# A decoder layer whose token blocks are turned by VectorE and DMA in place of TensorE

## The chip, the core and the metric

The kernel runs on one core of one Trainium2 chip. The metric is the device time of one execution in microseconds (us), as the median of several runs. The kernel before took 3067.01 us (three runs, 3065.17 to 3067.51).

A core has five engines with instruction queues of their own: TensorE (PE in the profile; its weight loads are PEld), VectorE (DVE), ScalarE (ACT), GpSimd (POOL) and SyncE (SP, which here only issues DMAs). They meet through semaphores. Sixteen DMA engines carry out what SP, ACT and POOL issue. SBUF is the on-chip memory, with 128 partitions; PSUM is the memory that TensorE writes its products to, in banks.

## The reference: what is computed

One decoder layer in float32, with layer normalization after each part. `x` has 32 sequences of 64 tokens with 512 features, so 2048 tokens.

```python
x = _layernorm(x + attn(x, ...))            # 32 heads on 8 key/value heads of 128; keys and values: 512 gathered
                                            # cache rows and the 64 tokens of the first sequence
x = _layernorm(x + xattn(x, ctx_4096, ...)) # each sequence attends to its own 64 context tokens
z = x @ W.T + b                             # feed-forward with 8 experts of rank 16, folded into one product
m = einsum(x, A, B, p_scores)
x = _layernorm(z + minimum(0.5 * norm(z) / (norm(m) + 1e-6), 1.0) * m)
```

## The kernel before

**Tokens and blocks.** The 2048 tokens are four blocks (`tb`, 0 to 3) of 512. A block is held twice. `acc[tb]` has tokens on the partitions: `[128, 4, 512]`, four row groups `j` of 128 tokens with 512 features each; token `j * 128 + p` of the block lies on partition `p` (`rows`, L111). The turned copy, `xTs` in the first stage and `xT[tb]` (x1T) later, has features on the partitions: `[128, 4, 512]`, four feature groups `c` of 128 and 512 tokens each. TensorE contracts over partitions, so each product that reads x needs the turned copy. The first one is laid out on the host (`xT_in`). x after the first and after the second normalization (x1 and x2) has to be turned on the chip.

**How x is turned before.** `transpose_rows` (L125) takes one row group: four TensorE transposes of 128x128 into one PSUM bank (L129), and a copy of 128x512 to the turned tile by ScalarE or VectorE (L131).

**Stages.** (1) *Self attention* (`scores`, `move`, `values`; to about 1830 us). (2) *Keys and values of the context* (L986 to L1031): 15 pairs `(gp, tb)` of two heads and one block. Each pair is a product of seven steps in the order `KV_ORDER = (1, 6, 5, 7, 2, 4, 3)`. A step is 12 matmul groups into the banks x, y or z (L395 to L410), of which there are two sets, taken in turn; `read` then lets VectorE add what a step left (L417). Steps 6, 7 and 4 add up in the same bank y, and each of their partial sums is read before the next is added. After each step one entry of the list `fill` is issued (L1017), which spreads other work over the pair: for `gp == 1` the statistics and the scaling of the first normalization, for `gp == 2` the four turned row groups of x1, one behind each of the first four steps. After the pair, `store_kv` writes two 512 KB tiles to DRAM (L472); these tiles have two buffers. (3) *Cross attention*: 32 units `(g, tb)` of four heads and one block. Unit `n` issues its queries, turns its weights with VectorE's 32x32 transposes (L1104) and eight DMAs that move the 32x32 blocks between partitions (`move`, L1118), and in the next iteration `attend` multiplies them with the values (`pox`, L1139) and empties four PSUM banks into `oT` with the value bias added (ScalarE L1157, VectorE L1159, four instructions of 128x256 each). `output_sums` on GpSimd (L266) and the output product `wx` (L292) read `oT`. (4) *Feed-forward*: `feed_forward(tb)` (L1193), woven in at the end. Its weight loads take 128 token columns of `xT[tb]` and of `uT` (L1204, L1210, L1211).

**x2.** When the last unit of a block is projected (L1171), its statistics are taken, ScalarE scales it (L167), and `transpose_block` goes to the list `later`, which is emptied between step 2 and step 4 of the next queries (L1298). Blocks 0 and 1 fall into the iterations of units 30 and 31, blocks 2 and 3 into the time after them.

**What sets the order.** In stage 2 TensorE and VectorE run in the order in which the code issues (`manual_schedule`, L990); in stage 3 TensorE, GpSimd and VectorE do, without VectorE from the last unit on (L1277). Elsewhere a planner orders an engine's instructions by priority. Semaphores are set by the framework: an instruction waits until what it reads is written and until what it overwrites has been read, and a tile of a tag with one buffer is handed on when all uses of the one before it are over.

```python
for i in KV_ORDER:                 # L1014
    pr.step(i)                     # TensorE
    pr.read()                      # VectorE: the additions of this step
    if fill:
        fill.pop(0)()              # one entry of other work
```

Of the kernel before, what the change touches and what calls it, by code (L numbers as in the profile page):

```python
# [9 lines left out]
F32 = mybir.dt.float32  # L10
I32 = mybir.dt.int32
AF = mybir.ActivationFunctionType
ALU = mybir.AluOpType
# [3 lines left out]
P = 128  # L17
DIM = 512
NH, NKV, HD = 32, 8, 128
REP = NH // NKV  # L20
NT = 2048
SEQ = 64
TB = 512
NTB = NT // TB
TPB = TB // P
NC = DIM // P
# [5 lines left out]
SQ = 32  # L32
NQD = P // SQ
# [19 lines left out]
def decoder_layer(  # L53
# [30 lines left out]
    nc = tc.nc  # L84
# [12 lines left out]

    acc = [act.tile([P, TPB, DIM], F32, tag=f"acc{b}", name=f"acc{b}") for b in range(NTB)]  # L100
    xT = []

# [6 lines left out]
        )  # L109

    def rows(src, tb):  # L111
        return src[tb * TB : (tb + 1) * TB, :].rearrange("(j p) f -> p j f", p=P)


    psum = []
# [17 lines left out]
    def transpose_block(tb, name):  # L133
        for j in range(TPB):
            transpose_rows(acc[tb][:, j, :], xT[tb], j, f"{name}_{tb}_{j}")

    def layernorm(tb, name):
        for part in layernorm_parts(tb, name):
# [47 lines left out]
    HF = DIM // 2  # L186
# [290 lines left out]
    later = []  # L477


    with ExitStack() as ph:  # L480
# [4 lines left out]
        sb = ph.enter_context(tc.tile_pool(name="sa", bufs=2))  # L485
# [76 lines left out]
        def rotate(g, t0=0, t1=NKT):  # L562
# [14 lines left out]
            nc.gpsimd.tensor_tensor(k4[:, :, :, 1], k4[:, :, :, 1], tmq, ALU.subtract)  # L577
            nc.vector.tensor_tensor(k4[:, :, :, 0], k4[:, :, :, 0], tmp, ALU.add)

        x64 = kc.tile([P, NC, SEQ], F32, name="x64")  # L580

        def new_keys(g):

            wk, wv = wkv_cur.pop(g)
            src = xTs[0] if g == 0 else x64
            kTs[g] = kv.tile([P, NKEY], F32, tag="kT", name=f"kT{g}")
            new = bank([P, 1, TB], f"new{g}", "po1")[:, 0, :]
            pk, pv = new[:, :SEQ], new[:, P : 2 * P]  # L590
            for c in range(NC):
                nc.tensor.matmul(
                    pk, wk[:, c, :], src[:, c, :SEQ], start=(c == 0), stop=(c == NC - 1),
                    skip_group_check=True,
                )
            for c in range(NC):
                for i in range(2):
                    nc.tensor.matmul(
                        pv[i * SEQ : (i + 1) * SEQ, :], src[:, c, :SEQ], wv[:, c, :],
                        start=False, stop=(c == NC - 1), skip_group_check=True,  # L600
                    )
            nc.scalar.activation(
                kTs[g].rearrange("p (s b k) -> p s b k", s=2, k=SQ)[:, :, SHARED, :],
                pk.rearrange("p (s k) -> p s k", s=2), AF.Copy, scale=nrm2,
            )
            nc.scalar.copy(vs[g][:, NKT, :], pv)
# [169 lines left out]
        t = {i: big.tile([P, 2, HF], F32, tag=f"tx{i}", name=f"tx0_{i}") for i in range(1, 5)}  # L776
        for j in range(NKT):
            gather_keys(0, j)
        nc.vector.tensor_tensor(t[1], q[0, 1], q[0, 0], sub)
        nc.vector.tensor_tensor(wq0[7], wq0[1], wq0[5], sub)  # L780
        nc.vector.tensor_tensor(wq0[5], wq0[5], wq0[4], ALU.add)
# [13 lines left out]
        c = first.c  # L795
# [9 lines left out]
        for j in range(NKT):  # L805
            gather_values(0, j)
        cached_keys(0, "s0")
        nc.gpsimd.tensor_copy(x64, xTs[0][:, :, :SEQ])
        nc.vector.tensor_tensor(t[3], q[1, 1], q[0, 1], sub)
        nc.vector.tensor_tensor(t[4], q[1, 0], t[2], sub)  # L810
        tok[1] = token_sums(xTs[1], "tx1", nc.gpsimd)
# [151 lines left out]
    with ExitStack() as ph:  # L963
# [23 lines left out]
        with ExitStack() as st:  # L987
            ke = st.enter_context(tc.tile_pool(name="ke", bufs=1))
            psum.append(st.enter_context(tc.tile_pool(name="kps", bufs=1, space=PSUM)))
            st.enter_context(tc.manual_schedule(  # L990
                engines={mybir.EngineType.PE, mybir.EngineType.DVE}
            ))
            for tb in range(2, NTB):
                encT[tb] = ke.tile([P, NC, TB], F32, tag=f"encT{tb}", name=f"encT{tb}")
                load_features(encT[tb], encT_in, tb)
            kvw[1] = load_kv_left(1, "wo")
            fill, turns = [], [0]

            def rows_turn(src, dst, j, name):
                transpose_rows(src, dst, j, name, f"t{turns[0] % 2}")  # L1000
                turns[0] += 1

            pairs = [(gp, tb) for gp in range(NKV // 2) for tb in range(NTB)][1:]
            for k, (gp, tb) in enumerate(pairs):
                if gp == 1:
                    stats, scale = layernorm_parts(tb, "a")
                    fill += [lambda: None, stats, lambda: None, scale]
                if gp == 2:
                    fill += [lambda tb=tb, j=j: rows_turn(
                        acc[tb][:, j, :], xT[tb], j, f"x1_{tb}_{j}") for j in range(TPB)]  # L1010
                tiles = [ke.tile([P, 2, 2, HF], F32, tag=f"c{i}", name=f"c{gp}_{tb}_{i}", bufs=2)
                         for i in range(2)]
                pr = keys_values(gp, tb, tiles, {z: f"{z}{k % 2}" for z in "xyz"})
                for i in KV_ORDER:  # L1014
                    pr.step(i)
                    pr.read()
                    if fill:  # L1017
                        fill.pop(0)()
                if gp == 0 and tb < NTB - 1:
                    encR[tb + 1] = token_sums(  # L1020
                        encT[tb + 1], f"te{tb + 1}", nc.gpsimd, ke, f"te{tb + 1}_"
                    )
                store_kv(gp, tb, tiles)
                if tb == NTB - 1 and gp < 2:
                    kvw[gp + 2] = load_kv_left(gp + 2, ("wq", "wo")[gp])
                if tb == NTB - 1 and gp == 2:
                    load_xq(0)
                if gp == 3 and tb == 0:
                    right[0] = token_sums(xT[0], "txx0", nc.gpsimd)
            load_xo(0)  # L1030
            psum.pop()  # L1031
# [92 lines left out]
        def attend(n):  # L1124

            g, tb = units[n]
            oTs[n] = output_tiles(f"oTx{g}_{tb}")
            o5 = [o.rearrange("d h (t b q) -> d t b h q", t=TPB, b=2) for o in oTs[n]]
            po = {}
            for pr in range(2):  # L1130
                for b in range(2):
                    name = f"pox{g}_{tb}_{pr}_{b}"
                    po[pr, b] = (bank([P, 2, REP * SEQ], name) if pr else
                                 pp.tile([P, 2, REP * SEQ], F32, tag=f"po{b}", name=name))
                for i in range(2):
                    for b in range(2):
                        r = slice(b * SEQ, (b + 1) * SEQ)
                        t = 2 * pr + i
                        nc.tensor.matmul(  # L1139
                            po[pr, b][:, i, :].rearrange("d (h a j) -> d h a j", h=REP, a=2),  # L1140
                            kvs[n][r, pr, 1, i * HD : (i + 1) * HD],
                            pTs[n][r, :, t * P : (t + 1) * P].rearrange(
                                "p a (h j) -> p h a j", h=REP
                            ),
                            start=True, stop=True,
                        )

            bias = bv[:, g : g + 1]
            for pr in range(2):
                for j in range(2):  # L1150
                    for b in range(2):
                        dst = o5[j][:, 2 * pr : 2 * pr + 2, b, :, :]
                        src = po[pr, b][:, :, j * HF // 2 : (j + 1) * HF // 2].rearrange(
                            "d i (h q) -> d i h q", h=2
                        )
                        if b == 0:
                            nc.scalar.activation(dst, src, AF.Identity, bias=bias)  # L1157
                        else:
                            nc.vector.tensor_scalar(dst, src, bias, None, ALU.add)  # L1159
            left = output_sums(oTs.pop(n), f"sox{g}_{tb}")  # L1160
            pjs[n] = Projection(left, wo_cur[g], tb, f"wx{g}_{tb}", XYZ)
            del pTs[n], kvs[n]

        def project(n, *steps):
            g, tb = units[n]
            for i in steps:
                pjs[n].step(i)
                pjs[n].read()
            if steps[-1] == 4:
                del pjs[n]  # L1170
                if g == NKV - 1:  # L1171
                    stats, scale = layernorm_parts(tb, "x", by_act=True)
                    stats()
                    scales.append(scale)
                    later.append(lambda: transpose_block(tb, "x2"))


        def load_ffn():
# [14 lines left out]
        def feed_forward(tb):  # L1193
# [7 lines left out]
            nc.vector.tensor_scalar(uT, pu, pe, None, ALU.mult)  # L1201
            for i in range(TPB):
                u = f"{tb}_{i}"
                cols = slice(i * P, (i + 1) * P)  # L1204
                a = acc[tb][:, i, :]
                pz = bank([P, DIM], f"pz{u}")
                pm = bank([P, DIM], f"pm{u}")
# [19 lines left out]
                nc.vector.tensor_scalar(gam, gam, CLAMP, 1.0, ALU.mult, ALU.min)  # L1227
                nc.vector.scalar_tensor_tensor(a, pm, gam, a, ALU.mult, ALU.add)
                layernorm_tile(tb, i, "f")
                r0 = tb * TB + i * P  # L1230
                nc.sync.dma_start(out=out[r0 : r0 + P, :], in_=a)

        def next_tokens(n, part):

# [163 lines left out]
```

## Time and profile before

| what | value |
|---|---|
| median of the runs | 3067.01 us |
| the profiled execution | 3067.85 us |
| its span, first to last instruction | 3066.1 us |
| TensorE busy, matmuls | 3028.1 us, 99% |
| VectorE / ScalarE / GpSimd busy | 2171.1 / 766.4 / 961.1 us |
| mean granted TensorE clock | 0.999 |
| DMA: queue of SP | 186224 packets, 280.60 MB, 33.2% of 16 engines |
| transposes of x1 and x2 on TensorE (L129) | 128, 1937.4 to 3032.2 us |
| copies out of their banks (L131) | ACT 0.585 to 0.617 us, DVE 0.680 to 0.682 us each in stage 2 |

An engine is "busy" while an instruction of it runs; matmuls overlap, so the sum of their durations is more than the time in which they are issued, and their slots are read from their start times. A line of a timeline gives start and length in us, engine, line of the code, operation, the tiles (written `out<-in`), the shape, and how many in a row (x4); a bracket is the idle time of that engine before it and what ended it. TensorE's instructions in float32 come in two passes, so a matmul of the code counts twice (a transpose counts once). "SPq" lines are DMA issues on SyncE's queue; their length runs from the first issue to the end of the last.

### The profile page before, as it was taken

To read this page: it belongs to the slowest core of one execution; us is meant where nothing else is said; L and a number is where in the kernel's file an instruction comes from. 1 tells how busy PE (TensorE), PEld (TensorE's weight loads), DVE (VectorE), ACT (ScalarE), POOL (GpSimd) and SP (SyncE) were. 2 spreads that over 40 slices of the span, in tenths; PEclk is the share of its full clock that TensorE was granted. 3 is DMA by queue.
4 is the path that set the end of the run, shared out by engine and by line. 5 is a ranking of instruction groups with operands and counts; after the bars stand their busy time and mean duration, and the time that the engine had idled before them with its cause. 6 is when DMAs were issued, how large, how long until landed. Compare 5 with 4: busy or idle time off the path is not lost.

```text
span 3066.1 us, 42299 instructions
## 1 busy us (share of the span) xinstructions
PE 3028.1 (99%) x14944; PEld 2317.9 (76%) x14944; DVE 2171.1 (71%) x3945; ACT 766.4 (25%) x1776; POOL 961.1 (31%) x789
## 2 busy tenths in 40 slices
PE   8999999999999999999999999999999999999998
PEld 6677777777767777777777769988888888888864
DVE  7787787777877877877877764436666656666677
ACT  2323222222322233232222221211111111111232
POOL 4221321321321321322322123036434444444421
PEclk9999999999999999999999999999999999999999
DMA  5444444444344354344344343231121121121101
GB/s 173 128 132 129 109 116 128 107 122 119 104 125 118 102 130 119 101 128 120 101 125 113 91 129 141 99 108 50 55 62 52 52 66 51 51 69 49 49 28 42
DMA packets 201105, 298.66 MB, mean 97 GB/s; under 512 B 44352, under 2 KB 95040, under 8 KB 200896
## 3 DMA queue, kind: packets, MB, share of 16 engines
q1 hardware_dynamic: 186224, 280.60, 33.2%
q10 hardware_dynamic: 12624, 11.16, 1.3%
q0 software_dynamic: 2048, 4.20, 0.5%
q8 instruction: 120, 1.97, 0.3%
q14 instruction: 89, 0.73, 0.1%
HBM read 107.05 MB, written 20.97 MB: 42 GB/s over the span
## 4 chain that ended last, share of the span: by engine, by line
PE 91%; DVE 4%; SPq 2%; DMA 1%; ACT 1%; issue 1%; ACTq 0%; DVEq 0%
PE po L677 15%; PE s L631 14%; PE sx L1068 2%; PE pox L1139 2%; SPq L669 2%; PE wx_2y L292 1%; PE w_0y L292 1%; PE wx_1y L292 1%; PE wx_0y L292 1%; PE w_3y L292 1%; PE qx_3y L292 1%; PE qx_2y L292 1%; PE qx_0y L292 1%; PE q_2y L292 1%; PE wx_3y L292 1%; PE qx_1y L292 1%
## 5 line engine op out<-in xcount | busy, mean ns | idle before, releaser
L639 ACT ACTIVATE p<-s,nmax 128x576 f32<-128x576 f32 x512 | 379.1, 741 | 1244.9 <-DVE nmax L636 1234.8
L631 PE MATMUL s<-kT,qT 128*128 128x288 f32 x2048 | 576.5, 407 | 5.0 <-ACT p L639 4.2
L677 PE MATMUL po<-pT,v 128*128 128x512 f32 (+1 forms) x1280 | 549.0, 602 | 6.4 <-DMA pT<-T 6.0
L631 PEld LDWEIGHTS s<-kT,qT 128*128 128x128 f32 x2048 | 387.2, 190 | 108.0 <-issue 18.7
L636 DVE TENSOR_REDUCE nmax<-s 128x1 f32<-128x576 f32 x512 | 384.1, 750 | 59.2 <-PE s L631 59.2
L657 DVE STREAM_TRANSPOSE T<-p 128x576 f32<-128x576 f32 x512 | 394.2, 770 | 4.9 <-DVE nmax L636 0.5
L677 PEld LDWEIGHTS po<-pT,v 128*128 128x128 f32 (+1 forms) x1280 | 213.3, 189 | 206.5 <-issue 177.8
L649 DVE TENSOR_SCALAR p<-p,den 128x576 f32<-128x576 f32 x512 | 319.9, 625 | 17.9
L648 DVE RECIPROCAL den<-den 128x1 f32<-128x1 f32 x512 | 83.9, 164 | 230.0 <-ACT p L639 219.9
L266 POOL TENSOR_TENSOR so<-oT,oT 128x512 f32<-128x512 f32 x32 | 40.7, 1271 | 553.0 <-ACT oT L700 553.0
L268 POOL TENSOR_TENSOR so<-oT 128x512 f32<-128x512 f32 x32 | 40.6, 1270 | 346.2 <-ACT oT L700 95.7
L1247 POOL TENSOR_TENSOR txx<-x1T 128x512 f32<-128x512 f32 x31 | 39.3, 1267 | 229.9 <-PE qx_3z L292 93.2
L207 POOL TENSOR_TENSOR tx<-xT 128x512 f32<-128x512 f32 x31 | 39.6, 1278 | 206.3 <-PE q_3z L292 65.0
L639 ACT ACTIVATION_READ_ACCUMULATOR p<-s,nmax 128x1 f32 x512 | 98.7, 193 | 0.0
L266 POOL TENSOR_TENSOR sox<-oTx,oTx 128x512 f32<-128x512 f32 x32 | 40.5, 1265 | 181.5 <-DVE oTx L1159 176.0
L1085 ACT ACTIVATE ex<-ex 128x512 f32<-128x512 f32 x64 | 39.3, 630 | 203.2 <-DVE ex L1084 203.2
L1068 PEld LDWEIGHTS sx<-kvx,qTx 128*64 128x64 f32 x2048 | 62.3, 138 | 10.6 <-issue 10.6
L700 ACT COPY oT<-po 128x512 f32<-128x512 f32 x128 | 68.2, 587 | 4.7 <-PE po L677 3.8
L1157 ACT ACTIVATE oTx<-pox,bv 128x256 f32<-128x256 f32 x128 | 52.0, 470 | 66.4 <-PE pox L1139 66.4
L1068 PE MATMUL sx<-kvx,qTx 128*64 128x64 f32 x2048 | 66.7, 224 | 0.0
L1139 PE MATMUL pox<-pTx,kvx 64*128 64x256 f32 x512 | 64.6, 389 | 0.0
L1159 DVE TENSOR_SCALAR oTx<-pox,bv 128x256 f32<-128x256 f32 x128 | 53.6, 479 | 9.9 <-PE pox L1139 9.9
(447 smaller groups left out, 5767.6 us busy)
## 6 DMA issues: line engine op xcount, KB each, us to landing
pT<-T SPq DMA_DIRECT2D x1016, 80.0 KB
pT<-T SPq DMA_DIRECT2D x1008, 64.0 KB
xT<-in_xT SPq DMA_DIRECT2D x31, 1024.0 KB
kvx<-kv SPq DMA_DIRECT2D x32, 512.0 KB
pTx<-Tx SPq DMA_DIRECT2D x256, 64.0 KB
kv<-c SPq DMA_DIRECT2D x30, 512.0 KB
wo<-in_woT SPq DMA_DIRECT2D x32, 256.0 KB
xwq<-in_xwq SPq DMA_DIRECT2D x32, 256.0 KB
```

The lines of the kernel that those rows point to most:

```text
L266: nc.gpsimd.tensor_tensor(t[1], a[1, 0], a[1, 1], ALU.add)
L292: nc.tensor.matmul(self.banks[b][:, m, :], self.left[i][:, k, m * P : (m + 1) * P], self.right[i][:, k, :], start=(first and m + k == 0), ...
L631: nc.tensor.matmul(s[:, a, :HALF], qTs[n // REP][:, units[n][2], i * P : (i + 1) * P], kTs[g][:, a * HALF : (a + 1) * HALF], start=True, s ...
L636: nc.vector.tensor_reduce(nmax, s[:, :, :HALF], AX.XY, ALU.max, negate=True)
L639: nc.scalar.activation(p.rearrange("q (a k) -> q a k", a=2), s[:, :, :HALF], AF.Exp, bias=nmax, accum_out=den,)
L648: nc.vector.reciprocal(den, den)
L649: nc.vector.tensor_scalar(p, p, den, None, ALU.mult)
L657: nc.vector.transpose(Ts[n][:, :, i, :], ps_.pop((n, i)).rearrange("q (b k) -> q b k", k=SQ))
L677: nc.tensor.matmul(pos[n].rearrange("d (a q) -> d a q", a=NQD), vs[units[n][0]][rows, v, :], pTs[n // 2][rows, :, chunk, :], skip_group_ch ...
L700: nc.scalar.copy(o[:, i, :].rearrange("d (t a k) -> d a t k", t=TPB, a=NQD), pos.pop(n - 1 + i).rearrange("d (a t k) -> d a t k", a=NQD, t ...
L1068: nc.tensor.matmul(s[b * SEQ : (b + 1) * SEQ, i * REP + h, :], qTs[n][:, h, pr * HF + c0 : pr * HF + c0 + SEQ], kvs[n][:, pr, 0, c0 : c0 + ...
L1139: nc.tensor.matmul(po[pr, b][:, i, :].rearrange("d (h a j) -> d h a j", h=REP, a=2), kvs[n][r, pr, 1, i * HD : (i + 1) * HD], pTs[n][r, :, ...
```

## The change

- **Token order.** A partition of `acc` now holds four tokens that follow each other: token `4 * p + j` of the block is on partition `p` in row group `j` (`rows`). The host lays out `xT_in` in the order (j, p) to match, the output DMA writes by `rows`, and `x64`, the first sequence's 64 tokens, is picked out of the new order; it is now copied before the first use of it (group 0 read `xTs[0]` directly before).
- **x1, all four blocks.** `rows_turn` is replaced. Each row group is turned by one VectorE transpose of 32x32 blocks into a tile `room` `[128, 16, 32, 4]`, at every fourth element (`turn_rows`). When the four groups are in, sixteen DMAs on SyncE's queue move 32 partitions each to 32 partitions of x1T, four pieces of 512 bytes a partition (`move_rows`, 64 KB each). The fifth entry of `fill` issues them. `room` comes from the pool `ke`, whose tiles have one buffer.
- **x2, blocks 0 and 1.** The same, with a `room` of one buffer in the pool of stage 3. Blocks 2 and 3 are still turned by TensorE.
- **x1T and x2 of blocks 0 and 1** are thereby in the plain token order, x2 of blocks 2 and 3 in the order (j, p). So `attend` has to write `oT` in the order (j, p): each eviction is split in two, 16 instructions of 128x128 in place of 8 of 128x256 per unit, and each writes with a step of 128 elements. `feed_forward` loads its weights from every fourth column for blocks 0 and 1.

```diff
     def rows(src, tb):
-        return src[tb * TB : (tb + 1) * TB, :].rearrange("(j p) f -> p j f", p=P)
+        return src[tb * TB : (tb + 1) * TB, :].rearrange("(p j) f -> p j f", p=P)
...
+    def turn_rows(src, room, j):
+        nc.vector.transpose(room[:, :, :, j], src.rearrange("p (b f) -> p b f", f=SQ))
+
+    def move_rows(room, dst):
+        blocks = room.rearrange("f (c r) t j -> f r c (t j)", r=NQD)
+        for a in range(NQD):
+            for r in range(NQD):
+                nc.sync.dma_start(
+                    out=dst[r * SQ : (r + 1) * SQ, :, a * P : (a + 1) * P],
+                    in_=blocks[a * SQ : (a + 1) * SQ, r, :, :],
+                )
...
-            src = xTs[0] if g == 0 else x64
...
+        nc.gpsimd.tensor_copy(
+            x64.rearrange("p c (j k) -> p c j k", j=TPB),
+            xTs[0].rearrange("p c (j k) -> p c j k", j=TPB)[:, :, :, : SEQ // TPB],
+        )
...
                 if gp == 2:
-                    fill += [lambda tb=tb, j=j: rows_turn(
-                        acc[tb][:, j, :], xT[tb], j, f"x1_{tb}_{j}") for j in range(TPB)]
+                    room = ke.tile([P, DIM // SQ, SQ, TPB], F32, tag="room", name=f"room{tb}")
+                    fill += [lambda tb=tb, j=j, room=room: turn_rows(
+                        acc[tb][:, j, :], room, j) for j in range(TPB)]
+                    fill.append(lambda tb=tb, room=room: move_rows(room, xT[tb]))
...
-            o5 = [o.rearrange("d h (t b q) -> d t b h q", t=TPB, b=2) for o in oTs[n]]
+            o5 = [o.rearrange("d h (q t b k) -> d t b h k q", t=TPB, b=2, q=TPB) for o in oTs[n]]
...
-                        dst = o5[j][:, 2 * pr : 2 * pr + 2, b, :, :]
-                        src = po[pr, b][:, :, j * HF // 2 : (j + 1) * HF // 2].rearrange(
-                            "d i (h q) -> d i h q", h=2
-                        )
-                        if b == 0:
-                            nc.scalar.activation(dst, src, AF.Identity, bias=bias)
-                        else:
-                            nc.vector.tensor_scalar(dst, src, bias, None, ALU.add)
+                        for i in range(2):
+                            dst = o5[j][:, 2 * pr + i, b, :, :, :]
+                            src = po[pr, b][:, i, j * HF // 2 : (j + 1) * HF // 2].rearrange(
+                                "d (h k q) -> d h k q", h=2, q=TPB
+                            )
+                            if b == 0:
+                                nc.scalar.activation(dst, src, AF.Identity, bias=bias)
+                            else:
+                                nc.vector.tensor_scalar(dst, src, bias, None, ALU.add)
...
-                    later.append(lambda: transpose_block(tb, "x2"))
+                    if tb < 2:
+                        later.append(lambda: turn_block(tb))
+                    else:
+                        later.append(lambda: transpose_block(tb, "x2"))
+
+        def turn_block(tb):
+            room = sb.tile([P, DIM // SQ, SQ, TPB], F32, tag="room", name=f"room2_{tb}", bufs=1)
+            for j in range(TPB):
+                turn_rows(acc[tb][:, j, :], room, j)
+            move_rows(room, xT[tb])
...
-                cols = slice(i * P, (i + 1) * P)
+                cols = slice(i, None, TPB) if tb < 2 else slice(i * P, (i + 1) * P)
...
-                r0 = tb * TB + i * P
-                nc.sync.dma_start(out=out[r0 : r0 + P, :], in_=a)
+                nc.sync.dma_start(out=rows(out, tb)[:, i, :], in_=a)
...
-        "xT": g["x"].reshape(NT, DIM).T,
+        "xT": g["x"].reshape(NTB, P, TPB, DIM).transpose(3, 0, 2, 1).reshape(DIM, NT),
```

More of the change, by code (lines that the diff above doesn't have):

```diff
@@ L592, in new_keys @@
                 nc.tensor.matmul(
-                    pk, wk[:, c, :], src[:, c, :SEQ], start=(c == 0), stop=(c == NC - 1),
+                    pk, wk[:, c, :], x64[:, c, :], start=(c == 0), stop=(c == NC - 1),
                     skip_group_check=True,
@@ L598, in new_keys @@
                     nc.tensor.matmul(
-                        pv[i * SEQ : (i + 1) * SEQ, :], src[:, c, :SEQ], wv[:, c, :],
+                        pv[i * SEQ : (i + 1) * SEQ, :], x64[:, c, :], wv[:, c, :],
                         start=False, stop=(c == NC - 1), skip_group_check=True,
@@ L807, in decoder_layer @@
         cached_keys(0, "s0")
-        nc.gpsimd.tensor_copy(x64, xTs[0][:, :, :SEQ])
         nc.vector.tensor_tensor(t[3], q[1, 1], q[0, 1], sub)
@@ L996, in decoder_layer @@
             kvw[1] = load_kv_left(1, "wo")
[L997 to L1001, printed above, removed]
+            fill = []
             pairs = [(gp, tb) for gp in range(NKV // 2) for tb in range(NTB)][1:]
```

## The prediction, made before the changed kernel was run

> **What bounds the kernel now.** I read the page's busy times first, then TensorE's own waits, and after that the timelines around the transposes that go.
>
> ```profile
> span 3066.1 us, 42299 instructions
> ...
> PE 91%; DVE 4%; SPq 2%; DMA 1%; ACT 1%; issue 1%; ACTq 0%; DVEq 0%
> ```
>
> The last line is the chain that ended last: 91% of it is TensorE, and TensorE is busy for 99% of the span. An instruction taken from it is worth its slot, as long as nothing new makes it wait. So two questions decide: how long the slots are, and what waits on what takes their place.
>
> The timeline of TensorE in the keys-and-values stage, for the first block of x1 (start, length):
>
> ```profile
> 1937.49 0.60 PE L129 MATMUL x<-ident,acc 128*128 128x128 f32 x4
> 1937.92 1.03 PE L400 MATMUL kv_0y<-te,xwkv 128*128 128x256 f32 x4
> ...
> 1942.31 1.03 PE L400 MATMUL kv_0y<-te,xwkv 128*128 128x256 f32 x4
> ```
>
> Four transposes hold TensorE from 1937.49 to 1937.92: 0.43 us, not the 0.60 that they are listed with, since matmuls overlap. A step without transposes takes 1.76 us (1946.26 to 1948.02 in the same answer), a pair of seven steps 12.3 us, and with four turns 14.04 us (1935.73 to 1949.77).
>
> The same view in the cross attention, where block 0 of x2 is turned:
>
> ```profile
> 2892.40 1.89 PE L292 MATMUL qx_2x<-x1T,xwq 128*128 128x256 f32 x8
> 2894.13 0.60 PE L129 MATMUL x<-ident,acc 128*128 128x128 f32 x4
> 2895.22 1.13 PE L129 MATMUL x<-ident,acc 128*128 128x128 f32 x8 [0.49 <-ACT qTx L328]
> 2896.66 0.66 PE L129 MATMUL x<-ident,acc 128*128 128x128 f32 x4 [0.31 <-DVE x1T L131]
> 2897.15 1.89 PE L292 MATMUL qx_2y<-txx,xwq 128*128 128x256 f32 x8
> ```
>
> Here sixteen transposes cost 2894.13 to 2897.15, 3.0 us, because they wait for the copies that empty their banks (the brackets).
>
> **What is removed.** Keys-and-values stage: 16 groups by 0.435 us = 7.0 us; TensorE was busy for all 55 us from 1937 to 1992, so all of it is on the path. x2 of blocks 0 and 1: 3.0 us each (block 1: 2925.66 to 2928.69), 6.0 us. Blocks 2 and 3 stay. In all 13.0 us.
>
> **What is added: the turn of x1.** Each block gets four VectorE transposes into `room` and then sixteen DMAs on SyncE's queue. `room` has one buffer. So the first turn of the next block must wait until the sixteen moves of this one have landed. VectorE keeps its written order here: behind that turn stands the addition L417 of step 6, and TensorE's step 7 adds into the bank that this addition reads. That is a new wait on the path. The rows that price it:
>
> ```profile
> 1939.94 0.69 DVE L417 TENSOR_TENSOR c<-kv_0y,c 128x512 f32<-128x512 f32 x1 [3.31 <-PE kv_0y L406]
> ...
> 1944.32 0.69 DVE L417 TENSOR_TENSOR c<-kv_0y,c 128x512 f32<-128x512 f32 x1 [3.10 <-issue]
> ...
> 2061.33 1.30 DVE L1104 STREAM_TRANSPOSE Tx<-ex 128x512 f32<-128x512 f32 x2
> ...
> 2062.66 4.95 SPq L1118 DMA_DIRECT2D pTx<-Tx  x8
> ...
> 2068.70 2.43 PE L1139 MATMUL pox<-pTx,kvx 64*128 64x256 f32 x16
> ```
>
> A turn of 128x512 costs 0.65 us (the pair in 1.30). Step 7 takes 2.01 us from its first matmul (1942.31) to the addition behind it (1944.32). Eight moves of 64 KB, 32 partitions to 32, leave SyncE in 4.95 us, one per 0.63. The first reader of the last one, issued near 2067.0, starts at 2068.70, so it landed within 1.7 us; the chain of waits has 2.6 us for one at 80.01. I take 2.0.
>
> From the start of a block's first turn to that of the next: turn 0.65, addition 0.69, step 7 to its addition 2.01, two additions 1.22, fourth turn 0.69, fifteen issue intervals 9.5, landing 2.0 = 16.8 us. TensorE's pair is 12.3. Each of the three boundaries between blocks so stalls TensorE for 4.5 us: 13.5 us. The moves carry four 512-byte pieces a partition, where the rows have one of 2 KB. The trace has no such move. Its issue lies between 0.48 us (xwkv, two pieces on 128 partitions: four in 1.90 at 1761.96) and 1.1 us (xT, four pieces on 128: 10.63 to the next at 11.74); I take 0.63, of the row with the same 32 partitions on chip. At 0.48 a stall is 2.2 us, at 1.1 it is 11.5.
>
> A stall this long touches the clock. By the windows view TensorE's granted clock averages 0.89 over 3056 to 3060 and 0.50 after: it halved near 3059.1, 3.9 us after the last matmul ended. At the start eight matmuls take 3.75 us instead of 1.89, and full speed is reached some 9 us after the first. A stall of 4.5 us is just beyond 3.9, so it may or may not halve. A slow step 7 costs 1.8 us; the rest of a slow stretch only eats the next stall, except after the last one (up to 4.7 us). Between 0 and 8.3 us; I take 2.5, about one halving.
> [...]
>
> **Other parts that I cost at nothing.** (1) *x2 blocks 0 and 1*: eight turns and 32 moves. VectorE has them at 2894.2 to 2896.8, in place of two copies; the additions and evictions behind them end about 0.3 us later, inside the room measured next. The moves hold SyncE for 10 us, to about 2907; behind them stand kvx, whose scores come an iteration later, and pTx, issued at 2917.44 today. The second use of their room comes 28 us after the first. Without cover: 1 to 2 us a block.
> (2) *Evictions of pox*: 8 instructions of 256 elements become 16 of 128, 32 times.
>
> ```profile
> 2098.93 1.67 DVE L1159 TENSOR_SCALAR oTx<-pox,bv 128x256 f32<-128x256 f32 x4 [0.30 <-PE pox L1139]
> 2101.19 1.05 PEld L292 LDWEIGHTS wx_1x<-xwo,oTx 128*128 128x128 f32 x5
> ```
>
> VectorE's four start 0.40 us apart. Halved, they cost 0.20 (all by element) to 0.40 (all fixed) each; at 0.28 the sixth of eight, the last that the first product needs, ends at 2100.7, before the weight load at 2101.19. At 0.40 it is 0.2 late, 31 times: 6 us. GpSimd starts its sums 0.6 later and has 1.9 to spare before wx_0y (2074.8 against 2076.73).
> (3) *Strided access*: the evictions write 512 bytes apart, the turns 16 bytes, and the feed-forward loads weights 16 bytes apart. The widest single-element step in the trace is 8 bytes: L575 writes it in 0.28 us, L574 without a step in 0.29. That row is nearest, so zero. From the other side: at double cost per element the sixth eviction ends near 2101.4 to 2101.5, 0.3 late, 9 us in 31 units; a weight load of 190 ns hides under matmuls 430 ns apart, and at fourfold 80 loads cost 0.33 each, 26 us. Below nothing: no row gives a gain.
> [...]
> (4) *Kv stores* queue behind moves by up to 10 us; their tiles have two buffers, so a store has a pair's 12 us or more. (5) *x64 copied earlier on GpSimd*: its gathers end at 9.04, it then waits for a DMA until 13.15, the copy takes 0.53, the matmuls that read it start at 16.95. If late: 0.5 us.
>
> **Sum.** -7.0 - 6.0 + 13.5 + 2.5 = +3.0 us. The profiled execution took 3067.85 us (span 3066.1 and 1.75 around it), 0.8 above the runs' median. 3067.85 + 3.0 = 3071.
>
> **The rivals.**
> *The moves keep up* (0.27): SyncE issues them at 0.48 or faster, or they land sooner. Three stalls of 2.2 us: -13.0 + 6.6 = -6.4, 3061; without any stall -13, 3055. For it: SyncE has rows at 0.48. Against: all rows from 32 partitions to 32 stand at 0.63, whatever their bytes (64 or 80 KB). The stall vanishes only under 0.33.
> *A move costs by its pieces* (0.12; slower): 1.1 us as xT's four pieces. Stalls of 11.5 us, 34.5, with the clock's 8.3: +30, 3097. It makes the kernel slower beyond doubt from about 0.75 us a move (stalls 6.3 us each, +6 before the clock).
> *Stride bites* (0.14): evictions 9 us, weight loads up to 26, on top of +3: 3080 to 3105. It decides once an eviction of 128 costs over 0.37 us.
> *The forecast* (0.47): 3063 to 3082, from 0.51 us a move with no halving to 0.75 with all.
>
> That the change doesn't do what it says I give nothing: the transposes leave the stream in the diff.
>
> **Chances.** A difference under 0.2%, 6.1 us, is about what a measurement of this kernel cannot tell from none. Slower by more: 0.17 of the forecast's 0.47, 0.12, and 0.13 of stride's 0.14: 0.42. Faster: 0.22 of the first rival's 0.27. Within: 0.30, 0.05 and 0.01: 0.36. The range for 8 in 10: from a stall-free KV stage nearly whole, 3055, to dear moves nearly whole, 3095.
>
> **What would show it.** Right: the VectorE turn `room<-acc` of blocks 1 to 3 idles some 7 us for the DMA `x1T<-room`, and TensorE's kv y matmuls idle about 4.5 us three times for L417; sixteen moves take 10 us of SyncE; the stage's four pairs take about 6 us more than 56; x2's two blocks are 3 us shorter each; the rest is unmoved. Wrong: no wait of VectorE for that DMA; a move interval far from 0.63; a granted clock that stays at 1.0 or falls in all three gaps; oTx evictions over 0.37 us with TensorE waiting at wx; pz weight loads over 430 ns.

## The result, and the profile after

The changed kernel takes 3081.89 us (median of six runs, 3079.95 to 3085.24); the kernel before, run beside it, 3067.28 us (3065.17 to 3069.44). The ratio is 1.0047, with a 95% interval of 1.0037 to 1.0058: 14.6 us slower, where 3071 with 3055 to 3095 was predicted. The profiled execution took 3082.88 us. Its page, span and chain that ended last:

```profile
span 3081.1 us, 42488 instructions
...
PE 92%; DVE 4%; SPq 1%; issue 1%; ACT 1%; DMA 1%; ACTq 0%; DVEq 0%
```

TensorE still carries the chain. The page alone hides what changed: VectorE's share of the chain is the same 4%. The waits of TensorE show it (line, tile and releaser; then us in total, times, longest):

```profile
PE kv_1y L416 <- DVE c L433: 5.7, 1, 5.7
PE kv_3y L416 <- DVE c L433: 5.5, 1, 5.5
...
PE kv_2y L416 <- DVE c L433: 5.0, 1, 5.0
```

Three waits of TensorE for an addition of VectorE (L433 is L417 of before), one at each boundary between blocks. And what VectorE waited for, from the waits of that engine:

```profile
DVE room L141 <- DMA x1T<-room: 24.9, 3, 8.6
```

The same place as a timeline (start, length, engine):

```profile
1947.07 10.33 SPq L148 DMA_DIRECT2D x1T<-room  x16
...
1953.96 1.05 PE L422 MATMUL kv_1z<-xwkv,te 128*128 128x128 f32 x8
...
1959.10 1.08 DVE L141 STREAM_TRANSPOSE room<-acc 128x512 f32<-128x512 f32 x1 [8.62 <-DMA x1T<-room]
1960.03 0.67 DVE L433 TENSOR_TENSOR c<-kv_1y,c 128x512 f32<-128x512 f32 x1
...
1960.75 0.79 PE L416 MATMUL kv_1y<-te,xwkv 128*128 128x256 f32 x1 [5.73 <-DVE c L433]
```

Read it upwards: step 7 (1960.75) waits for an addition (1960.03), that stands behind a turn (1959.10), that waits for sixteen moves of the block before, issued from 1947.07 to 1957.40. TensorE's last work had ended at 1955.01.

Where the time went, by the start times of the same matmuls in both traces: stage 2 is 7.0 us shorter for the transposes, 16.8 longer for the three waits (16.2 of it is the idle time in the view above; the rest is the overlap of a matmul with the one before it, which a wait takes away), and 8.2 longer because the granted clock falls by half for 6.83 us behind each wait (2.7 or 2.8 us each). The windows view shows the middle of the first one (us, busy time of each engine, PEclk, DMA share, GB/s):

```profile
1953.00:1960.00 7.00, 2.02 (x15) 1.72 (x13) 0.90 (x1) 0.00 (x0) 0.00 (x0) 0.95 0.58 169
1960.00:1967.00 7.00, 6.25 (x25) 5.51 (x26) 4.92 (x7) 0.00 (x0) 0.00 (x0) 0.56 0.17 66
```

x2 is 2.97 and 2.95 us shorter, and gives 0.72 and 0.56 back in two new waits (the idle time alone is 0.6 and 0.4):

```profile
PE wx_1x L308 <- DVE oTx L1178: 0.6, 1, 0.6
PE wx_2x L308 <- DVE oTx L1178: 0.4, 1, 0.4
```

-7.0 + 16.8 + 8.2 - 4.6 = +13.4 us. The two profiled executions differ by 15.0; the rest, 1.6 us, lies at the end of stage 1, whose products there the change left as they were: one wait for a `pT` DMA was 3.0 us, against 1.8 in the kernel before, and the clock fell behind it. The last section comes back to it.

### The profile page after: what moved, and what is told of

It is laid out like the page before. It is cut to its first block, busy times and chain, and to the rows that moved or that the text cites. A ratio compares the mean times of both kernels' runs of the same rounds, so it can differ in the third digit from the quotient of the medians.

```text
span 3081.1 us, 42488 instructions
## 1 busy us (share of the span) xinstructions
PE 3027.9 (98%) x14848; PEld 2324.4 (75%) x14848; DVE 2196.4 (71%) x4085; ACT 782.2 (25%) x1892; POOL 966.9 (31%) x789
## 4 chain that ended last, share of the span: by engine, by line
PE 92%; DVE 4%; SPq 1%; issue 1%; ACT 1%; DMA 1%; ACTq 0%; DVEq 0%
PE po L693 16%; PE s L647 15%; PE sx L1085 2%; PE pox L1157 2%; PE w_0y L308 1%; PE q_2y L308 1%; PE q_3y L308 1%; PE wx_2y L308 1%; PE w_2y L308 1%; PE wx_0y L308 1%; PE w_3y L308 1%; PE qx_0y L308 1%; PE wx_1y L308 1%; PE wx_3y L308 1%; PE qx_1y L308 1%; PE qx_2y L308 1%
## 5 line engine op out<-in xcount | busy, mean ns | idle before, releaser
L1176 ACT ACTIVATE oTx<-pox,bv 128x128 f32<-128x128 f32 x256 | 73.5, 484 | 63.6 <-PE pox L1157 63.6
L1178 DVE TENSOR_SCALAR oTx<-pox,bv 128x128 f32<-128x128 f32 x256 | 72.4, 419 | 9.0 <-PE pox L1157 9.0
```

## The experiments

Theory A: the one `room` turns ten microseconds of DMA issue into a wait of VectorE, this into one of TensorE, and this into a slow clock. Theory B: the access at a step of 16 bytes and the moves' traffic cost by themselves, and the wait is only where it shows. Unless said otherwise each is a patch of the changed kernel. Each was timed beside the kernel before on the same chip, which took 3067.0 to 3067.5 us there.

**Two rooms.**

```diff
-  room = ke.tile([...], F32, tag="room", name=f"room{tb}")
+  room = ke.tile([...], F32, tag="room", name=f"room{tb}", bufs=2)
...  (bo and bz are allocated, and bo loaded, behind the stage)
```

> The changed kernel with two rooms in stage 2 in place of one (two bias tiles are set up after the stage to make space for it); turns, moves and everything else stay. Theory A (the one room makes the first turn wait for the 16 moves of the block before, TensorE waits for VectorE, and each wait halves the clock): the three waits of 5.7, 5.0 and 5.5 us and the three stretches at half clock (8.2 us) all go, so 3081.9 - 25 = about 3057, at most 1 us a block more where four turns of 1.1 us still make an addition late. Theory B (the turns' writes at a step of 16 bytes and the 64 moves slow the stage themselves, the wait for the room is only where it shows): nothing that costs is taken away, 3079 to 3083.

3056.79 us (3054.41 to 3058.33), ratio to before 0.9963 (0.9950 to 0.9977). 25.1 us less than the changed kernel, and the trace had put 16.8 + 8.2 = 25.0 on waits and clock. In its timeline of VectorE the second block's first turn has no bracket:

```profile
1948.66 0.69 DVE L433 TENSOR_TENSOR c<-kv_0z,c 128x512 f32<-128x512 f32 x1 [1.06 <-PE kv_0z L422]
1949.27 1.10 DVE L141 STREAM_TRANSPOSE room<-acc 128x512 f32<-128x512 f32 x1
```

The turns are as long as before (1.10 us), the moves as many. TensorE waits for none of them in this stage, and the clock line of the page has a 9 (90% or more of full speed) in the slice where the changed kernel's has an 8. Theory A holds, B falls.

**Half of the moves on ScalarE's queue.**

```diff
-                nc.sync.dma_start(
+                queue = nc.scalar if split and r % 2 else nc.sync
+                queue.dma_start(
```

> The changed kernel with one room as it is, but every second one of stage 2's 16 moves a block is issued by ScalarE's queue. Theory A: the issue of the moves takes 8 x 0.65 = 5.2 us in place of 10.3, so VectorE's wait falls from 8.6 to about 3.5 us and TensorE's waits from 5 to 6 us to 0 to 1 us, too short for the clock to fall: 3081.9 - 16 - 8 + (0 to 3) = 3057 to 3061. If eight issues of 0.65 us on ScalarE hold up its copies out of PSUM, up to 3 us a block comes back: 3061 to 3070. Theory B (the moves' traffic and the strided turns cost): 3079 to 3083.

3068.07 us (3064.39 to 3071.32), ratio 1.0001 (0.9992 to 1.0010). The two queues, and ScalarE's next copy:

```profile
1946.69 5.19 SPq L149 DMA_DIRECT2D x1T<-room  x8
1946.70 5.53 ACTq L149 DMA_DIRECT2D x1T<-room  x8
```
```profile
1952.34 0.47 ACT L430 ACTIVATE c<-kv_1x,bk 128x256 f32<-128x256 f32 x1 [5.71 <-DMA x1T<-room]
```

Issue was halved as planned, and 13.8 us came back of 25. But the next turn starts 3.4 us after the last issue in place of 2.4 (the profile names the store of kv, which goes out beside the moves, as what ended last), so VectorE still waits 4.8 us and TensorE 1.9, 2.9 and 2.0. I had expected 0 to 1 us, too short for the clock to fall. Behind the first wait, of 1.93 us, it did not: four matmuls of 256 columns take 1.13 us there. But of the 11.3 us above two rooms alone the three waits are 6.8, and the mean granted clock is 0.997 in place of 0.998. By these figures I estimate that it fell behind the other two. That part of the expectation was wrong, and gave the next question.

**Work in the gap.**

```diff
                 for i in KV_ORDER:
+                    if gp == 2 and tb > 0 and i == 7:
+                        idle = bank([P, TB], f"idle{tb}", "t0")
+                        for _ in range(4):
+                            nc.tensor.matmul(idle, ident, encT[2][:, 0, :], start=True, stop=True)
                     pr.step(i)
```

> The changed kernel with work added: four products of 512 columns (about 0.84 us each, twice a row of 256 columns at 0.42) go to a PSUM bank that nobody reads, ahead of step 7 in the three pairs where TensorE waits for VectorE. The wait still ends when it did, but TensorE's empty time in it falls from 5 to 6 us to about 2. Theory A with the clock (the empty time lets the clock fall by half for 6.83 us, which costs 2.7 us each time): three stretches at half clock go, 3081.9 - 8.2 = 3073.7. Rival (the fall of the clock has another cause, such as the moves or the load before it): the stretches stay, 3081 to 3083.

3077.44 us (3076.38 to 3078.72): 4.5 us faster with work added, about half of what was expected. The second pair's timeline of TensorE says why:

```profile
1971.11 3.60 PE L1035 MATMUL idle<-encT,ident 128*128 128x512 f32 x8
1977.15 1.94 PE L416 MATMUL kv_2y<-te,xwkv 128*128 128x256 f32 x4 [2.44 <-DVE c L433]
```

Four matmuls of 256 columns take 1.94 us where they take 1.13 behind the first pair's gap of 2.30 us. A gap of 2.44 us still halved the clock (granted share 0.55 from 1977.0 to 1980.5 us), one of 2.30 did not, though with two rooms alone shorter ones did: behind waits of 1.51 and 1.70 us four matmuls of 288 columns take 2.29 us at 59.02, where they took 1.24 at 56.08. The gap's length alone doesn't decide. In the changed kernel's profile the falls of this stage begin at 1959.26, 1979.74 and 2000.22 us, each six times 3.41 us behind the one before; this grid led to the next run:

```diff
-                        for _ in range(4):
+                        for _ in range(6):
```

> The changed kernel with six products that nobody reads ahead of step 7 in place of four (5.1 us in place of 3.4). With four, TensorE was idle for 2.3, 2.4 and 2.7 us, and the clock still fell for 3.41 us after the second and the third. Laid over all profiles so far, the falls begin on a grid of 3.41 us, behind those intervals of the grid in which TensorE was idle for over about 1.8 us. With six the idle time is 0.6 to 1.0 us in each: no fall in stage 2, 3077.4 - 2.5 = 3075 within 2. If any idle time there lets the clock fall, it stays at 3077.

3074.65 us (3073.31 to 3076.22), as forecast: idle times of 0.6, 0.7 and 1.1 us; four matmuls of 256 columns take 1.13 us behind each of the first two, and the mean granted clock is 0.998, where it is 0.997 with four products. What the clock cost the changed kernel is thereby measured: 7.2 us, with nothing taken away but idle time of TensorE. It is less than the 8.2 us of the trace, since at full clock TensorE comes to the next wait sooner: VectorE now waits 8.62 and 8.76 us for the room at the first two boundaries, not 8.62 and 7.91. This run also shows the chain between two blocks at full clock, one step after the other:

```profile
1955.82 1.10 DVE L141 STREAM_TRANSPOSE room<-acc 128x512 f32<-128x512 f32 x1 [8.62 <-DMA x1T<-room]
...
1957.36 2.00 DVE L141 STREAM_TRANSPOSE room<-acc 128x512 f32<-128x512 f32 x2
1959.62 0.69 DVE L433 TENSOR_TENSOR c<-kv_1y,c 128x512 f32<-128x512 f32 x1 [0.26 <-PE kv_1y L422]
...
1960.95 1.13 DVE L141 STREAM_TRANSPOSE room<-acc 128x512 f32<-128x512 f32 x1
...
1974.27 1.09 DVE L141 STREAM_TRANSPOSE room<-acc 128x512 f32<-128x512 f32 x1 [8.76 <-DMA x1T<-room]
```
```profile
1962.11 10.25 SPq L148 DMA_DIRECT2D x1T<-room  x16
```

From turn to turn 18.45 us, where 16.8 was predicted.

**x2 alone, x1 alone.**

```diff
-                    if tb < 2:
+                    if tb < 0:          # x2 by TensorE in all blocks; weight columns to match
```

> The changed kernel with x2's blocks 0 and 1 by TensorE's transposes again, x1 by turns and moves as changed. By the trace the two x2 blocks gave 2.97 + 2.95 us and took back 0.72 + 0.56, so they are worth 4.6 us: 3086.5. Rival (VectorE's eight turns of 1.1 us and the 32 moves in the last units cost as much as the transposes saved): 3081 to 3083.

3086.79 us (3083.09 to 3087.36): 4.9 more, where the trace had said 4.6.

```diff
-                    fill += [lambda tb=tb, j=j, room=room: turn_rows(...) ...]
-                    fill.append(lambda tb=tb, room=room: move_rows(room, xT[tb]))
+                    fill += [lambda ...: rows_turn(acc[tb][:, j, :], xT[tb], j, ...) ...]
...                    (rows_turn of before, but: eng(dst[:, :, j::TPB], pt))
```

> x1 by TensorE's transposes as before (evicted into every fourth column, since the tokens lie four a partition), x2's blocks 0 and 1 by turns and moves as changed. Stage 2 should stand as before the change, so the time before less what x2 gives by the trace: 3067.3 - 4.6 = 3062.7. If the new order of the tokens itself costs (evictions at a step of 512 bytes, other loads), 3064 to 3070.

3063.97 us (3062.63 to 3066.87), ratio 0.9990 (0.9981 to 0.9999). The 3062.7 expected lies within the interval; the median is 1.3 us above it, at the foot of the 3064 to 3070 that a cost of the new order was to give, so a cost of about that size is not ruled out. So the change is a gain of 3 to 5 us in x2 and a loss of 18 to 19 us in x1. Its other parts (16 evictions of 128 in place of 8 of 256, weight loads at a step of 16 bytes, the new order of x64) cost no more than these runs spread (3062.6 to 3066.9), beyond what they do to x2.

**Turns that write runs of 32.**

```diff
-  rearrange("(p j) f -> p j f", p=P)                  # rows: token 4 p + j
+  rearrange("(a j t) f -> a t j f", a=NQD, j=TPB)     # token a*128 + j*32 + t on partition a*32+t
-  nc.vector.transpose(room[:, :, :, j], ...)          # x1's turns
+  nc.vector.transpose(room[:, :, j, :], ...)
-  o5 = [o.rearrange("d h (q t b k) -> d t b h k q", ...)]
+  o5 = [o.rearrange("d h (b a r k) -> d r b h a k", ...)]   # 8 evictions of 256 again
```

> The changed kernel with another order of tokens on the partitions (partition a*32+t holds tokens a*128 + j*32 + t, j from 0 to 3), so that stage 2's turns write runs of 32 contiguous elements in place of single elements at a step of 16 bytes; still one room, the same 16 moves of the same size; the attention's evictions go back to 256 elements each. x2's turns stay strided. Theory A: a turn falls from 1.05-1.13 us to the 0.65-0.69 us of the attention's turns, and the chain from one block's first turn to the next one's holds four of them, so TensorE's three waits shrink by 0.9 to 1.7 us each and stay long enough for the clock to fall: 3081.9 - (3 to 5) = 3077 to 3079. Theory B (the stride is what costs): most of the loss of 25 us in stage 2 goes, 3057 to 3065.

3102.14 us (3099.2 to 3105.5): 20 us slower than the changed kernel, which neither theory had. The same with two rooms:

> Both repairs of stage 2: two rooms and turns that write runs of 32. With two rooms alone the kernel took 3056.8 us and TensorE did not wait for VectorE in stage 2 at all. Theory A: shorter turns then shorten nothing that TensorE waits for: 3056.8 within 1.5. Theory B (strided turns and evictions cost by themselves): 3050 to 3054.

3080.16 us (3075.86 to 3081.44), 23 us slower than two rooms alone. The waits of TensorE between 40 and 260 us, first in this run, then in the one with two rooms alone, show that the loss has nothing to do with turns:

```profile
PE po L695 <- DMA pT<-T: 12.9, 3, 6.7
PE s L649 <- ACT p L657: 4.5, 3, 3.2
```
```profile
PE s L647 <- ACT p L655: 3.9, 3, 1.7
PE po L693 <- DMA pT<-T: 1.5, 2, 1.3
```

By the start times of the same matmuls 17 us of it lie ahead of 260 us, in the first units of stage 1, where x is loaded, 256 KB at a time; some 3 us lie behind the last matmul, where the output is stored. In the new order a load of 128 rows is a pattern of 4 by 32 rows. In the changed kernel's trace, without that pattern, each of the ten loads issued from 104 to 233 us has 128 packets of 2 KB, whose starts spread over 0.9 to 1.7 us (5.1 in one), and 16 small ones of 4 bytes. Up to 260 us the queue that carries these loads moves the same 6.62 MB in 4832 packets in the run with runs and two rooms and in 5024 with two rooms alone: 192 fewer, 12 for each of the 16 loads, so by my estimate 4 small packets a load in place of 16. Their issue takes 0.54 us each in place of 0.33. I take it that such a load was carried out in fewer parts and more slowly, with the moves of `pT` waiting behind it (12.9 us in place of 1.5); why was not shown. My expectations had not counted a cost of this pattern. So x and the output were laid flat:

```diff
-  "x": g["x"].reshape(NT, DIM),
+  "x": g["x"].reshape(NTB, NQD, TPB, SQ, DIM).transpose(0, 2, 1, 3, 4).reshape(NT, DIM),
...  (rows: "(j p) f -> p j f" again; the output is put back into order in the same way)
```

> The kernel with two rooms and turns that write runs of 32 (3080.2 us), but with x and the output laid in DRAM in the new order of the tokens, so that a load or store of 128 rows is one flat pattern again and not four pieces of 32 rows (the rows are reordered outside the kernel). Theory: the loss of 23 us against two rooms alone came with those loads and stores, which stage 1's first units and the last store wait behind: it goes, 3056.8 within 1.5. Rival (the new order costs in the attention or in the first keys): 3075 to 3080.

3053.48 us (3051.25 to 3055.04), ratio 0.9955 (0.9941 to 0.9968): 26.7 us less than with the pieces, so the pattern of these loads and stores was the cause. It is also 3.3 us under two rooms alone, where at most 1.5 were expected. By the trace 1.3 of that are x2's two waits for `oTx`, which are gone with eight evictions in place of sixteen. The other 2 us are not the layout's by anything that the traces show. TensorE waits 0.9 us less for `pT` over the whole run (4.6 us in place of 5.5); with two rooms alone the clock was slow near 59 us, as the 2.29 us above show; and the mean granted clock is 0.998 in both. The ranges of the two kernels' runs overlap a little (3051.25 to 3055.04 here, 3054.41 to 3058.33 there). So theory A was a little too narrow: the halved evictions did cost 1.3 us, beside x2's turns.

> One room and turns that write runs of 32 (3102.1 us), with x and the output laid in DRAM in the new order as well. Then it differs from the changed kernel in the turns alone (0.70 us in place of 1.08) and the evictions. By the trace of that run TensorE's three waits were 5.0, 4.2 and 5.4 us in place of 5.7, 5.0 and 5.5, and stage 2 was 2 us shorter: 3081.9 - 2 = 3080 within 2. Theory B (the stride costs): 3057 to 3065.

3078.01 us (3076.21 to 3079.72), 3.9 less than the changed kernel. The view of the tile `room` has the turns (min, median, max in ns; the 1120 is one of x2's, which stay strided):

```profile
L143 DVE STREAM_TRANSPOSE room<-acc x24: 669/702/1120, 1934.6 to 2938.0; 128x512 f32<-128x512 f32 x24
```

A turn in runs is 0.4 us shorter, which is worth about a microsecond a block while the room is one, and nothing that the trace shows while there are two. The flat order with two rooms is the fastest kernel of this study, 13.5 us under the kernel before; with spread turns as well it was not tried.

**x2's turns spread, and one block more** (both with two rooms and the changed kernel's order of tokens).

```diff
-                        later.append(lambda: turn_block(tb))   # four turns at once, ahead of attend
+                        turn_block(tb)                         # puts four turns and the moves into a list
...
             parts(n, (largest, 0), (largest, 1), (exponentials, 0), (exponentials, 1))
+            next_turn()
...          (one more behind each of weights 0 and weights 1, the last and the moves behind move(n))
```

> Two rooms, and in the last units x2's four turns of a block are put one by one behind the parts of the softmax in VectorE's order, not all four ahead of the attention's evictions. The two waits that the turns cause there (0.73 and 0.57 us by the trace) go: 3056.8 - 1.3 = 3055.5. Rival (a turn of 1.1 us delays whatever stands behind it, so the wait only moves): 3056 to 3059, with new waits of TensorE in the last three units.

3054.92 us (3053.36 to 3057.31) against 3056.79: the median fits, but the ranges overlap, so that it is faster isn't shown by the times. In the trace both waits for `oTx` are gone, and one new wait of TensorE has come:

```profile
PE pm L1245 <- DVE uT L1235: 0.8, 1, 0.8
```

VectorE's turns push back what stands behind them: `uT` of block 0's feed-forward starts at 2943.04 us, where it started at 2941.11 with two rooms alone. So the rival was right in part, and from 2890 us to the last matmul the gain is 1.0 us, not 1.3.

```diff
-TURNED = 2
+TURNED = 3
```

> The kernel with two rooms and spread turns (3054.9 us), and x2's block 2 by turns and moves as well, its four turns behind the last unit's attention evictions. TensorE's 16 transposes of a block were worth 2.97 and 2.95 us for blocks 0 and 1: 3054.9 - 3.0 = 3052. Rival: block 2 is scaled so late that its 16 moves (10.3 us to issue and 2 to land) are not done when its feed-forward begins, or its turns hold up VectorE's last work: 3054 to 3060, with a wait of TensorE for x1T or for VectorE ahead of that feed-forward.

3057.89 us (3054.65 to 3061.59): the rival was right. The 16 transposes are gone, and 2.4 us with them, until here:

```profile
2972.24 2.09 PE L1245 MATMUL pm<-bm,uT 128*128 128x512 f32 x2 [3.45 <-DVE uT L1235]
```

Behind the last unit VectorE has evictions, the feed-forwards' small work and now four turns, the last of them right ahead of `uT`; TensorE waits 3.45 us for it, and the clock falls behind that gap too: the two matmuls behind it take 2.09 us, where the same two take 1.02 at 2958.78.

## Why the prediction was right, step by step

It was right in range and sign, and its mechanism is the one that the runs show: the wait for the one room. But of the 14.6 us its sum had 3.0, less than the 6.1 us that it said a measurement cannot tell from none; the terms were of the wrong size. That the time still lies inside the range, at the top of the forecast's own 3063 to 3082, is in part luck: that top was worked out from moves at 0.75 us, and the range's end from moves at 1.1, while they took 0.64. The stride rival's 3080 to 3105 holds 3081.9 as well; it is the two-rooms run that decides against it. And two of the prediction's own signs of being wrong came: the clock fell in all three gaps, and TensorE waited for `oTx`, whose evictions took 0.42 us, at two of the output products.

| term | predicted | measured |
|---|---|---|
| x1's transposes gone | -7.0 | -7.0 (16 times 0.44) |
| three waits of TensorE | +13.5 | +16.8 |
| slow clock behind them | +2.5 | +8.2 |
| x2, blocks 0 and 1 | -6.0 | -4.6 |
| stage 1 | 0 | +1.6; from -1.7 to +3.6 in the eight runs with the same stage 1 |

- *"The first turn of the next block must wait until the sixteen moves of this one have landed."* Right: 24.9 us of VectorE in three waits; with two rooms none, and 25.1 us gone.
- *The chain of 16.8 us.* 18.45 in the run without falls. The issue was right (10.25 us, about 0.64 a move; four pieces a partition cost no more than one, so the rivals at 0.48 and at 1.1 us are out). Short were the turns, priced by a row whose writes are contiguous (0.65; with a step of 16 bytes 1.05 to 1.14), and the landing, 2.0 against 2.35 to 2.5. Some 0.5 us for the fourth turn, 0.3 for the first with its addition, 0.5 for the landing and 0.1 each for the two additions, step 7 and the issue make up the difference.
- *The clock* is the step that failed most. "It halved 3.9 us after the last matmul ended" was taken from the end of the kernel as a threshold for a gap. It is none: the clock fell in all three gaps, of 5.0 to 5.7 us, and in the work-in-the-gap run behind 2.44 us. The term of 2.5 us, one halving, measured 8.2.
- *x2, "inside the room measured next".* 1.3 us too hopeful: four turns of 1.1 us ahead of the evictions, not of 0.65, made TensorE wait for `oTx` twice. It needed both, long turns and sixteen short evictions: spread turns alone removed these two waits (and brought one of 0.8 us behind them), and eight evictions removed them too.
- *Evictions at zero* otherwise held: 0.42 us each on VectorE by length, but 0.26 from start to start, and no matmul shifts in stage 3 ahead of x2's first turn (from 2062 to 2890 us TensorE stays 19.6 us behind the kernel before). *Weight loads at a step of 16 bytes at zero* held too: 308 ns each in the feed-forward of blocks 0 and 1, against 190 in that of blocks 2 and 3 without the step, hidden under matmuls 430 ns apart. The step of 16 bytes did make the turns longer (1.10 us, in runs of 32 elements 0.70) and these loads (by 0.12 us), but the 9 us that the stride rival put on the evictions did not come.

## What to carry to other kernels

Ask of a new buffer when it is free again, not only when it is full: one tile with ten microseconds of DMA issue behind it cost over three times what it replaced (25 us against 7), and a second one turned a loss of 15 us into a gain of 10. A stall of TensorE had a second price here, the clock behind it: 2.7 or 2.8 us for each of the waits of 5.0 to 5.7 us, and it was due behind one of 2.44 us too. When a layout is rearranged, look at every load and store that follows it: four pieces in the outermost dimension of a DMA cost more here (20 us with one room, 23 with two) than the whole change had lost.

## What the runs showed of the hardware

**The clock's falls lie on a grid.** In the changed kernel's record of the granted clock the falls ahead of the last matmul begin at 1788.60, 1959.26, 1979.74 and 2000.22 us: 50, 6 and 6 intervals of 3.41 us apart. Each of these slow stretches is 6.83 us long, two intervals. The fall behind the last matmul, at 3075.42 us, is 315 intervals on. I added up TensorE's idle time in each interval of this grid from 30 us to the last matmul, at full clock; in the kernel before, on the grid through its one fall (3059.08 us, behind the last matmul). In the changed kernel the interval ahead of the fall at 1788.60 has 1.77 us idle, and those ahead of the other three are idle throughout. The most idle intervals that no fall follows have 1.70 and 1.73 us there, and 1.70 and 1.76 in the kernel before. Two single gaps that lie across a border of the grid, 1.82 us in the kernel before (1.26 and 0.56 on the two sides) and 1.87 in the changed kernel (0.83 and 1.03), are followed by no fall. From these two profiles I estimate that about 1.8 us of idle time within one interval decided here; by this estimate a gap of 2.30 us can leave the clock full and one of 2.44 halve it, as with work in the gap, by where they lie on the grid. Ends of matmuls are modelled, so 1.76 and 1.77 can't be told apart, and no run tries the border by itself.

**Stage 1 differs between runs, probably for this reason.** A wait of TensorE for a `pT` DMA near 1788 us is 2.99 us long in the changed kernel, and the clock falls at 1788.60; in the kernel before it is 1.82 us, and there is no fall. Near 57 us, where TensorE waits for ScalarE, it is the same: 1.70 us in these two, and no fall; with two rooms alone 1.51 and 1.70 us, with two rooms and turns in runs 3.16 us, and four matmuls of 288 columns take 2.29 us behind them in both runs, where they took 1.24. Apart from the order of x's rows and the copy of `x64`, the code of that stage is the same in all of them. I take this as the reason for much of the spread between runs of one kernel (3065 to 3072 for the kernel before); that it is, was not tried by itself.

**Moves between partitions** of 64 KB, 32 partitions to 32, leave SyncE's queue at 0.64 us each with a partition's 2 KB in four pieces (sixteen in 10.25 us) and at 0.62 with one (eight in 4.95 us, the kernel before), and ScalarE's at about 0.69 (eight in 5.53 us); the last one lands about 2.4 us after its issue, and about 3.4 with two queues at work (there the profile names a store of kv, not a move, as the last to end).
